# Two layers of attention on 16 images: column sums from chunk probabilities added in place, a step later, and layer 1's weights loaded for each image

## The chip, the cores and the metric

The kernel runs on one core of one Trainium2 chip. The metric is the device time of one execution in microseconds (us), lower is better; the time of a kernel is the median of its runs. A profile is one further execution, taken by the hardware profiler, with its own time.

The engines are named as in the profile: PE (TensorE) with PEld (its weight loads), DVE (VectorE), ACT (ScalarE), POOL (GpSimd) and SP (SyncE, which issues all the large transfers).

## What is computed

The input is 16 images of 64 x 64 pixels and 256 channels, float32. Two residual layers follow each other, each on a group-normalised image:

```python
# layer 0: linear attention over all 4096 pixels, 8 heads of 32
q, k, v = split(gn(x) @ w_qkv)
q = softmax(q, over the head's 32 features) * SCALE
k = softmax(k, over the 4096 pixels)
x = x + (k^T v applied to q) @ w_out
# layer 1: each pixel attends to its 7 x 7 neighbourhood, 8 heads of 32
q, k, v = gn(x) @ Wq + bq, gn(x) @ Wk + bk, gn(x) @ Wv + bv
scores = q . (k of the 49 neighbours + position embedding)
x = x + sum(softmax(scores) * v of the 49 neighbours)
```

The group norm has 32 groups of 8 channels and takes mean and variance over the pixels of an image and the channels of a group. In layer 1 the first four heads have an embedding that depends on one image axis of the neighbour, the other four on the other axis.

## The kernel before, in words

**Stages.** The images are worked on one after the other (the loop at L872). For each image come layer 0 (`layer0`, L500: products with wqkv at L514, the context at L532, output weights, and the residual products at L587), the statistics for layer 1, positional products (L630), `values` (L669, v written to a padded copy in HBM), `keys_queries` for head group 0 (L695), the local attention of head group 0 (L929), `keys_queries` for head group 1 (L930) and the local attention of head group 1 (L953). A head group `hg` is four heads. The instructions of PE, ACT, DVE and SP run in the order in which the program writes them (`manual_schedule`, L860), and POOL's order is left to the scheduler; an engine that waits holds up all that is behind it in its queue.

**Local attention** (`local_attention`, L740). The image is cut into four units of 16 columns (`UNITS`, L41) for each head group, and the 64 rows into nine chunks of 8 key rows (of the padded image). A chunk c of keys meets the query rows `span(c)`, L746: 14 rows for c = 1 to 7, 8 rows for c = 0, 6 rows for c = 8. `scores` (L750) multiplies keys and queries into PSUM (L766) and ACT takes the exponential into a work tile `e` (L774): 128 partitions (8 key rows by 16 key columns, as two halves) by 4 heads x 16 query columns x up to 14 query rows. There is no division by the maximum.

`weighted` (L777) forms, for each half j of the query columns, two sums over the keys (L797): `outs[j]`, the values weighted by e, and `zs[j]`, the plain sums of e, by a product with a block of ones. Each takes four matmuls that lie side by side in four column tiles of PE, one for each head. A query row is met by two chunks, so all these products are added up in PSUM; the four banks are first set to zero by a product with zeros (L784). At the end of a unit `finish` (L805) turns zs (L810), copies outs (ACT, L811), and for each j takes the reciprocal of one column per head (L815, L816), turns it back (L817), multiplies (DVE, L821) and adds the result to the image (POOL, L830). `watch` (L450) adds the sums and reciprocals to running totals on POOL (L451), to find values out of range.

**The order of the steps** is written out by hand in the loop at L832. There are 20 steps, four units i by five groups g of two chunks (the last has one chunk). A step first issues the scores of its own group, then the weighted products of the group before it (`held`), then, if that group ended a unit, the loads of a later unit's values (`load_window`, L728) and `finish`; last `between(i, g)`, which holds the work that belongs to other stages:

- in head group 0 (`between0`, L917): the windows for head group 1, the output stores of a finished unit, the loads of half of the next image, one strip a step (L925), and that half's statistics (`strip_stats`, L473) in units 2 and 3;
- in head group 1 (`between1`, L935): the next image's token tiles, the output stores, the statistics of the other half in unit 1, the group norm's three parts (`group_steps`, L255, with PE products at L266 and L275 and the DVE copies of their results, L268 and L277) in the first three steps of unit 2, and the normalisation of two strips (L283) in unit 3.

The score tiles and the small products of the group norm share two pairs of PSUM banks, taken in turn (`next_bank` gives the next one), so a group-norm product uses a bank that scores need again soon.

**What lies in SBUF.** Wv, Wk, Wq and bv as given stay in SBUF from the start (`wv_sb`, `wk_sb`, `wq_sb`, `bv_sb`). For each image, scaled copies are written to `wv`, `wk` (the tile of `w2`), `wq` and `bv` (`scale`, L601; L892), since the norm's scale is folded into the weights. The work pool has four tiles (L439), which hold e and the intermediate results of other stages. The tail pool has two.

Of the kernel before, what the change touches and what calls it, by code (L numbers as in the profile page):

```python
# [10 lines left out]
F32 = mybir.dt.float32  # L11
# [9 lines left out]
W = 64  # L21
# [67 lines left out]
class Net:  # L89


    def __init__(self, tc, cp, io):
        nc = tc.nc
        self.tc, self.nc, self.cp, self.io = tc, nc, cp, io
        cpk = io["cpk"]

        def tile_of(shape, name):
            return cp.tile(shape, F32, tag=name, name=name)

        self.ident = ident = tile_of([P, P], "ident")  # L100
        make_identity(nc, ident)
        self.grp = tile_of([P, P], "grp")
        nc.sync.dma_start(self.grp, cpk[:, C_GRP : C_GRP + P])
        self.wqkv_sb = tile_of([P, 2, 3 * C], "wqkv")
        self.wout_sb = tile_of([P, 2, C], "wout")
        self.wk_sb = tile_of([P, 2, C], "wk")
        self.wv_sb = tile_of([P, 2, C], "wv")
        for dst, src in ((self.wqkv_sb, "w_qkv"), (self.wout_sb, "w_out"), (self.wk_sb, "wk"), (self.wv_sb, "wv")):
            nc.sync.dma_start(dst, io[src].rearrange("(k p) f -> p k f", p=P))
        self.bk_sb = tile_of([P, 2], "bk")  # L110
        nc.sync.dma_start(self.bk_sb, io["bk"].rearrange("(k p) -> p k", p=P), allow_slow_non_contiguous=True)
        self.bv_sb = tile_of([P, C], "bv")
        nc.sync.dma_start(self.bv_sb, io["bv"].partition_broadcast(P))

        self.ctx_bd = [tile_of([P, P], f"ctxbd{i}") for i in range(2)]
        self.blockdiag = tile_of([P, P], "blockdiag")
        nc.gpsimd.memset(self.blockdiag, 0.0)
        for h in range(4):
            nc.gpsimd.memset(self.blockdiag[HD * h : HD * (h + 1), HD * h : HD * (h + 1)], 1.0)
        self.neghalf = tile_of([P, 1], "neghalf")  # L120
        nc.gpsimd.memset(self.neghalf, -0.5)

    def positions(self, psum):
# [3 lines left out]
        self.wq_sb = cp.tile([P, 2, C], F32, tag="wq", name="wq_sb")  # L127
        nc.sync.dma_start(self.wq_sb, io["wq"].rearrange("(k p) f -> p k f", p=P))
# [5 lines left out]
        with tc.tile_pool(name="setup", bufs=1) as sp:  # L134
            emb_sb = sp.tile([P, 2, KS], F32, tag="emb", name="emb_sb")
            nc.sync.dma_start(emb_sb[:, 0], io["emb0"].rearrange("p a b -> p (a b)"))
            nc.sync.dma_start(emb_sb[:, 1], io["emb1"].rearrange("p a b -> p (a b)"))
            emb_bd = sp.tile([P, 2, 8, 4], F32, tag="embbd", name="emb_bd")
            nc.gpsimd.memset(emb_bd, 0.0)
            wqT = sp.tile([P, 2, C], F32, tag="wqT", name="wqT")  # L140
            for hg in range(2):
                for h in range(4):
                    rows = slice(32 * h, 32 * h + 32)
                    nc.vector.tensor_copy(emb_bd[rows, hg, :KS, h], emb_sb[rows, hg])
                emb = emb_bd[:, hg].rearrange("p a b -> p (a b)")
                pt = psum(f"wqT{hg}")
                for k in range(2):
                    nc.tensor.transpose(pt[:, k * P : (k + 1) * P], self.wq_sb[:, k, hg * P : (hg + 1) * P], self.ident)
                nc.vector.tensor_copy(wqT[:, hg], pt[:, :C])
                for k in range(2):  # L150
                    pe = psum(f"we{hg}{k}")
                    nc.tensor.matmul(pe[:, :32], wqT[:, hg, k * P : (k + 1) * P], emb, start=True, stop=True)
                    nc.vector.tensor_copy(self.wpos[:, k, 32 * hg : 32 * hg + 32], pe[:, :32])
                pb = psum(f"be{hg}")
                nc.tensor.matmul(pb[:32, :1], emb, self.biases[:, 2 + hg : 3 + hg], start=True, stop=True)
                for a in range(2):
                    p0 = 64 * a + 32 * hg
                    nc.vector.tensor_copy(self.biases[p0 : p0 + 32, 4:5], pb[:32, :1])

    def residues(self, psum):  # L160
# [6 lines left out]

        self.stat = tile_of([P, 2, W], "stat")
# [187 lines left out]
def attention_fast(tc, io, ok):  # L356
# [3 lines left out]
    with ExitStack() as ctx:  # L360
# [78 lines left out]
        work = ctx.enter_context(tc.tile_pool(name="work", bufs=4))  # L439
# [35 lines left out]
        def stats_tile(name):  # L475
            return small.tile([P, 2, NS, 6], F32, tag="st", name=name)
# [23 lines left out]
        def layer0(b, x, xn, mean, rstd, xtok, ready):  # L500
# [74 lines left out]
            cT = work_tile(f"cT{b}")[:, :512].rearrange("p (a c) -> p a c", c=P)  # L575
# [23 lines left out]
            return st  # L599

# [139 lines left out]
        def local_attention(b, hg, x, y, vw, after_scores, between):  # L740
# [36 lines left out]
            def weighted(t, c, e, vw):  # L777
                lo, hi = span(c)
                m = 16 * (hi - lo)
                if c == 0:  # L780

                    for i, to in enumerate(single):
                        rows = slice(32 * i, 32 * i + 32)
                        nc.tensor.matmul(to, zb[rows], zb[rows, :1].to_broadcast([32, 512]), start=True, stop=False)  # L784
                for j in range(2):
                    for to in (outs[j], zs[j]):
                        for h in range(4):
                            pl, ab = divmod(h, 2)
                            pr = e[:, ab, pl * m : (pl + 1) * m]
                            dst = to[h * HD : (h + 1) * HD]  # L790
                            if hg == 0:
                                pr = pr.rearrange("p (r w) -> p r w", w=16)[:, :, 8 * j : 8 * j + 8]
                                dst = dst.rearrange("p (r w) -> p r w", w=8)[:, lo:hi]
                            else:
                                pr = pr.rearrange("p (w r) -> p w r", w=16)[:, 8 * j : 8 * j + 8]
                                dst = dst.rearrange("p (w r) -> p w r", w=8)[:, :, lo:hi]
                            nc.tensor.matmul(  # L797
                                dst,
                                ones if to is zs[j] else vw[:, j, c, h * HD : (h + 1) * HD],
                                pr,  # L800
                                start=False,
                                stop=(c == NB - 1),
                            )

            def finish(t):  # L805
                r = [tail.tile([P, 2, 512], F32, tag="tail", name=f"r{b}_{hg}_{t}_{j}") for j in range(2)]
                for j in range(2):


                    nc.vector.transpose(r[j][:, 0], zs[j])  # L810
                    nc.scalar.copy(r[j][:, 1], outs[j])  # L811
                for j in range(2):
# [11 lines left out]
                    for s in (2 * t + j, (2 * t + j + 1) % NS):  # L824
                        for _, p0, m, w, view in pieces(s):

                            a, e = max(w, w0), min(w + m, w0 + 8)
                            if a < e:
                                xv, yv = (view(i[hg][:, strip(s)])[..., a - w : e - w] for i in (x, y))
                                nc.gpsimd.tensor_tensor(yv, xv, by_rows(add[:, :, a - w0 : e - w0], xv), ALU.add)  # L830

            groups = [(i, g) for i in range(4) for g in range(5)]  # L832
            held = None
            for step in range(len(groups) + 1):
# [6 lines left out]
                if held:  # L841
                    i, g, es = held
                    for c, e in es:
                        weighted(UNITS[i], c, e, vw[i])
                    if g == 4:
                        vw.pop(i)
                        if i + 2 < 4:
                            vw[i + 2] = load_window(b, hg, UNITS[i + 2])
                        finish(UNITS[i])
                    between(i, g)  # L850
                held = new


        wm = small.tile([P, 2], F32, tag="wm", name="wm")
        nc.vector.tensor_reduce(wm[:, 0:1], n.wv_sb.rearrange("p a b -> p (a b)"), AX.X, ALU.max, apply_absolute_value=True)
        nc.vector.tensor_reduce(wm[:, 1:2], n.bv_sb, AX.X, ALU.max, apply_absolute_value=True)
# [3 lines left out]
        with tc.manual_schedule(engines=ORDERED):  # L860
# [9 lines left out]
            for s in ORDER[:2]:  # L870
                normalise(xn, x, *gn, s)
            for b in range(B):  # L872
                more = b + 1 < B
                x, xn = halves(b)
                st = layer0(b, x, xn, *gn, xtok, 2)
                mean, rstd = n.group_stats(st, 1e-5, small, bank, f"1_{b}")
# [5 lines left out]
                scale(wv, n.wv_sb, rstd)  # L882
# [9 lines left out]
                nc.vector.tensor_tensor(bv, n.bv_sb, pv[:, :C], ALU.subtract)  # L892
                store_rings()
                for i, s in enumerate(KEYED):
                    values(b, s, x)
                    if i == 1:
                        scale(wk, n.wk_sb, rstd)
                        scale(wq, n.wq_sb, rstd)
# [18 lines left out]
                def between0(i, g):  # L917
                    if g == 4:
                        if i >= 2:
                            vw1[i - 2] = load_window(b, 1, UNITS[i - 2])  # L920
                        store_out(0, i)
# [7 lines left out]
                local_attention(b, 0, x, y, vw, lambda: load_rings(1), between0)  # L929
                keys_queries(b, 1, x)  # L930
                if more:
# [3 lines left out]
                def between1(i, g):  # L935
                    nonlocal steps
                    if g == 4:
                        if more and i >= 2:
                            xtok[i - 2] = load_tokens(b + 1, i - 2)
                        store_out(1, i)  # L940
# [12 lines left out]
                local_attention(b, 1, x, y, vw1, lambda: None, between1)  # L953
# [387 lines left out]
```

## Times and profile before

Of three runs the median is 6052.62 us (6047.84 to 6058.84).

| | |
|---|---|
| profiled execution, its own time | 6068.61 us |
| its span, first to last instruction | 6066.8 us |
| mean granted PE clock | 0.962 of full |
| head group 0's attention, first image | 295.7 to 367.5 us, PE busy 61.69 us |
| keys and queries of head group 1, first image | 367.5 to 395.1 us, PE busy 27.60 us |
| head group 1's attention, first image | 395.1 to 468.2 us, PE busy 63.01 us |
| busy in that stretch: DVE, ACT, POOL | 27.98, 36.49, 15.80 us |
| L797, products with ones, 112 and other columns | 18432 matmuls (records) |
| all transfers | 526.94 MB, 87 GB/s on the average |

How to read it. The page first gives the busy time of each engine as a share of the span, then the queues, and then the chain of work that ended last, followed back from the last instruction to what released it at each step. A group of instructions is shown as line, engine, operation, result <- inputs, partitions x elements and number; behind the first bar its busy time in us and the mean length of one in ns; behind the second the idle time of the engine just before it and what ended most of it. A float32 matmul leaves two records, so the numbers of L766 and L797 are twice those of the program. The waits list what an engine stood still for: the instruction that had to start, the one that released it, the total in us, how often, and the longest. "issue" stands for a wait that ends without any event that the profile has. The granted clock of PE is 1 or 0.5 at any moment; 0.962 is a mean.

### The profile page before, as it was taken

The numbers are of one execution on the slowest core, as the hardware profiler recorded it, in microseconds if no ns is written. First come the engines' busy times: TensorE is split into PE (matmuls) and PEld (weight loads), VectorE is DVE, ScalarE is ACT, GpSimd is POOL, SyncE is SP. The second block draws the span as 40 slices with busy tenths as digits, with TensorE's granted clock in tenths as the row PEclk, the third lists the DMA queues.
The fourth block names the chain that finished last, engine by engine and source line by source line (L and its number), as shares of the span: only waits on it lengthen the run. The fifth ranks groups of instructions, "written<-read, shape, count | busy, mean of one in ns | idle before, by whom it ended". The sixth has DMA issues, their size and how long they took to land.

```text
span 6066.8 us, 171741 instructions
## 1 busy us (share of the span) xinstructions
PE 5506.4 (91%) x76913; PEld 3771.3 (62%) x76913; DVE 2874.6 (47%) x5034; ACT 2254.7 (37%) x3233; POOL 1029.9 (17%) x1945
## 2 busy tenths in 40 slices
PE   3999999898999989999898999999989999898998
PEld 2575665656656566665666657566565665756666
DVE  2544545445354444455444554454544545445354
ACT  0252433515334152342524425143252433415334
POOL 2012120211202113021120201212022120111202
PEclk9999999999999999999999999999999999999999
DMA  4341723516244252443515435163350724417234
GB/s 112 76 104 37 133 80 79 115 45 129 59 96 104 48 121 59 102 104 66 110 44 114 99 74 103 37 129 84 73 112 31 144 66 83 104 39 141 59 76 82
DMA packets 737035, 526.94 MB, mean 87 GB/s; under 512 B 240400, under 2 KB 667664, under 8 KB 733712
## 3 DMA queue, kind: packets, MB, share of 16 engines
q1 hardware_dynamic: 736288, 515.86, 38.9%
q8 instruction: 605, 9.91, 0.7%
q14 instruction: 142, 1.16, 0.1%
HBM read 357.02 MB, written 158.73 MB: 85 GB/s over the span
## 4 chain that ended last, share of the span: by engine, by line
PE 88%; ACT 4%; issue 4%; DVE 2%; SPq 1%; DMA 0%; POOL 0%; ACTq 0%; DVEq 0%; POOLq 0%
PE pd L766 16%; PE ps L797 16%; PE pd L514 15%; PE pd L704 7%; PE ps L532 7%; PE ps L704 5%; ACT qq L619 4%; PE pd L587 4%; PE ps L678 4%; PE pd L678 4%; PE ps L587 4%; PE ps L630 2%; PE ps L546 2%; PE ps L784 1%; SPq L399 1%
## 5 line engine op out<-in xcount | busy, mean ns | idle before, releaser
L774 ACT ACTIVATE e<-pd 128x896 f32<-128x896 f32 (+2 forms) x1152 | 928.5, 839 | 1132.0 <-PE pd L766 1129.4
L766 PE MATMUL pd<-qq,kaug 64*64 64x140 f32 (+5 forms) x27648 | 1052.3, 294 | 218.4 <-ACT e L774 143.5
L766 PEld LDWEIGHTS pd<-qq,kaug 64*64 64x64 f32 x27648 | 923.8, 140 | 354.4 <-issue 163.6
L514 PE MATMUL pd<-wqkv,img 128*128 128x512 f32 x2048 | 923.3, 595 | 1.7 <-DVE img L283 1.6
L797 PE MATMUL ps<-e,vw 128*32 128x112 f32 (+1 forms) x18432 | 853.8, 260 | 63.4 <-issue 63.0
L797 PE MATMUL ps<-e,ones 128*32 128x112 f32 (+1 forms) x18432 | 846.5, 256 | 59.7 <-issue 59.2
L810 DVE STREAM_TRANSPOSE r<-ps 128x512 f32<-128x512 f32 x256 | 168.8, 696 | 1437.6 <-PE ps L797 1437.3
L451 POOL TENSOR_TENSOR others<-others,rc 128x16 f32<-128x16 f32 x256 | 113.1, 442 | 2981.5 <-DVE rc L815 2981.5
L518 ACT ACTIVATE eq<-pd 128x1024 f32<-128x1024 f32 x256 | 261.9, 1023 | 943.3 <-PE pd L514 943.3
L514 PEld LDWEIGHTS pd<-wqkv,img 128*128 128x128 f32 x2048 | 372.6, 191 | 380.6 <-issue 353.3
L797 PEld LDWEIGHTS ps<-e,vw 128*32 128x32 f32 x18432 | 502.9, 113 | 154.9 <-issue 117.7
L797 PEld LDWEIGHTS ps<-e,ones 128*32 128x32 f32 x18432 | 546.5, 114 | 72.4 <-issue 71.8
L619 ACT ACTIVATE qq<-ps,bias 32x512 f32<-32x512 f32 (+2 forms) x544 | 320.2, 622 | 718.1 <-PE ps L630 712.5
L521 DVE TENSOR_REDUCE qz<-eq 128x16 f32<-128x512 f32 x256 | 175.5, 685 | 830.5 <-ACT eq L518 830.5
L532 PE MATMUL ps<-xtok,eq 128*128 128x257 f32 x2048 | 486.1, 380 | 0.0
L532 PEld LDWEIGHTS ps<-xtok,eq 128*128 128x128 f32 x2048 | 386.1, 190 | 149.0 <-issue 107.1
L830 POOL TENSOR_TENSOR img<-img,r 128x320 f32<-128x320 f32 (+1 forms) x512 | 421.5, 844 | 164.8 <-DVE rc L815 163.5
L619 ACT ACTIVATE kaug<-pd,bias 32x512 f32<-32x512 f32 x256 | 173.7, 679 | 633.6 <-PE pd L704 630.7
L473 DVE BATCH_NORM_STATS2 st<-img 128x6 f32<-128x512 f32 x512 | 319.9, 677 | 66.1 <-DMA img<-in_xc 66.1
L621 DVE TENSOR_SCALAR qq<-ps,bias 32x512 f32<-32x512 f32 x384 | 309.3, 806 | 6.8
L524 POOL TENSOR_TENSOR eq<-eq,qr 128x512 f32<-128x512 f32 x256 | 274.7, 1073 | 30.7 <-DVE qr L523 1.2
L821 DVE TENSOR_TENSOR r<-r 128x512 f32<-128x512 f32 x256 | 222.3, 868 | 27.5 <-DVE r L817 0.5
(126 smaller groups left out, 6170.0 us busy)
## 6 DMA issues: line engine op xcount, KB each, us to landing
vw<-vpad SPq DMA_DIRECT2D x512, 288.0 KB
img<-in_xc SPq DMA_DIRECT2D x256, 256.0 KB
xtok<-in_xt SPq DMA_DIRECT2D x64, 1024.0 KB
out<-img SPq DMA_DIRECT2D x256, 256.0 KB
vpad<-v SPq DMA_DIRECT2D x112, 512.0 KB
qq<-pos SPq DMA_DIRECT2D x128, 256.0 KB
qq<-in_ring SPq DMA_DIRECT2D x128, 256.0 KB
pos<-qq SPq DMA_DIRECT2D x128, 112.0 KB
```

What stands on the lines that cost most here:

```text
L473: nc.vector.bn_stats(st[:, k, s], x[k][:, strip(s)])
L514: nc.tensor.matmul(ps[:, t], xn[k][:, n0 : n0 + P], n.wqkv_sb[:, k, : 2 * C], start=(k == 0), stop=(k == 1))
L532: nc.tensor.matmul(pc[hg][:, : C + 1], eq[p][:, t, C + hg * P : C + (hg + 1) * P], xtok[p // 4][:, 2 * (p % 4) + t], start=(p == 0 and t = ...
L587: nc.tensor.matmul(py[co], w2[:, hg, co * P : (co + 1) * P], qq[:, hg, strip(s)], start=(hg == 0), stop=(hg == 1),)
L619: nc.scalar.activation(dst, src, AF.Identity, bias=bias)
L621: nc.vector.tensor_scalar(dst, src, bias, None, ALU.add)
L678: nc.tensor.matmul(pi[:, t], x[k][:, n0 : n0 + P], wv[:, k], start=(k == 0), stop=(k == 1))
L704: nc.tensor.matmul(ps[a], wgt[:, k, hg * P : (hg + 1) * P], x[k][:, strip(pair[a])], start=(k == 0), stop=(k == 1),)
L766: nc.tensor.matmul(to, kaug[pl][rows, u, 8 * c : 8 * c + 8].rearrange("p r w -> p (r w)"), q, start=True, stop=True,)
L774: nc.scalar.activation(e, ps[:, :, : 2 * m], AF.Exp)
L797: nc.tensor.matmul(dst, ones if to is zs[j] else vw[:, j, c, h * HD : (h + 1) * HD], pr, start=False, stop=(c == NB - 1),)
L830: nc.gpsimd.tensor_tensor(yv, xv, by_rows(add[:, :, a - w0 : e - w0], xv), ALU.add)
```

## The change

Four things are changed.

1. **Sums of two chunks.** Two neighbouring chunks c - 1 and c share six query rows. Once both have been read by the weighted products, `both_chunks` adds those six rows of chunk c - 1's e (384 elements for each partition) into chunk c's, in place, on DVE for even c and on POOL for odd c. The product with ones (`summed`) is then made for 8 rows per chunk instead of up to 14 (the six and the two that only chunk c has; 2 rows for c = 0, 6 for c = 8), a step after the weighted products, starts PSUM afresh (so no zeros are needed for zs), and needs each row only once.
2. **The end of a unit.** `finish` is a generator that runs over three steps: the two transposes, then the chain of j = 0, then that of j = 1 with the unit's output stores (`stored`). It starts a step later, and ACT's copies of outs stay where they were. `between` is called a step later. The loop has three more steps at its end.
3. **Weights.** Wv with bv, Wk and Wq are no longer kept in SBUF. They are loaded from HBM for each image (`load_weights`) into the tiles that hold the scaled copies, and scaled in place: Wv and bv during head group 0's attention, Wk after layer 0, Wq after `keys_queries` of head group 1.
4. **Space.** The work pool has six tiles instead of four, the statistics tile one buffer instead of two, and layer 0's `ctx_bd` lies in a work tile.

The core of the diff:

```diff
-        work = ctx.enter_context(tc.tile_pool(name="work", bufs=4))
+        work = ctx.enter_context(tc.tile_pool(name="work", bufs=6))
...
-            return small.tile([P, 2, NS, 6], F32, tag="st", name=name)
+            return small.tile([P, 2, NS, 6], F32, tag="st", bufs=1, name=name)
...
+        def load_weights(to, name):
+            nc.sync.dma_start(to, io[name].rearrange("(k p) f -> p k f", p=P))
+            if name == "wv":
+                nc.sync.dma_start(bv, io["bv"].partition_broadcast(P))
...
+            def both_chunks(c, e, before):
+                r0 = 8 * c - 2 * PAD
+                part = rows_of(c, e, r0, 8 * c)
+                engine = nc.gpsimd if c % 2 else nc.vector
+                engine.tensor_tensor(part, part, rows_of(c - 1, before, r0, 8 * c), ALU.add)
...
-                    for i, to in enumerate(single):
-                        rows = slice(32 * i, 32 * i + 32)
-                        nc.tensor.matmul(to, zb[rows], zb[rows, :1].to_broadcast([32, 512]), start=True, stop=False)
+                    for i, to in enumerate(outs):
+                        rows = slice(64 * i, 64 * i + 64)
+                        nc.tensor.matmul(to, zb[rows], zb[rows, :1].to_broadcast([64, 512]), start=True, stop=False)
                 for j in range(2):
-                    for to in (outs[j], zs[j]):
...
+                    for h in range(4):
+                        v = vw[:, j, c, h * HD : (h + 1) * HD]
+                        products(outs[j], j, h, c, e, *span(c), v, start=False, stop=(c == NB - 1))
+
+            def summed(c, e):
+                r0, r1 = max(8 * c - 2 * PAD, 0), min(8 * c + 8 - 2 * PAD, W)
+                for j in range(2):
+                    for h in range(4):
+                        products(zs[j], j, h, c, e, r0, r1, ones, start=True, stop=True)
...
-            for step in range(len(groups) + 1):
+            held, late, ends, rs, before = None, None, [], {}, None
+            for step in range(len(groups) + 4):
...
                     for c, e in es:
-                        weighted(UNITS[i], c, e, vw[i])
+                        weighted(c, e, vw[i])
                     if g == 4:
+                        rs[i] = [tail.tile([P, 2, 512], F32, tag="tail", name=f"r{b}_{hg}_{i}_{j}") for j in range(2)]
+                        for j in range(2):
+                            nc.scalar.copy(rs[i][j][:, 1], outs[j])
...
-                        finish(UNITS[i])
-                    between(i, g)
-                held = new
+                if late:
+                    i, g, es = late
+                    for c, e in es:
+                        summed(c, e)
+                    if g == 4:
+                        ends.append(finish(i, UNITS[i], rs.pop(i)))
+                if held:
+                    for c, e in held[2]:
+                        if c:
+                            both_chunks(c, e, before)
+                        before = e
+                for end in list(ends):
+                    if next(end, True):
+                        ends.remove(end)
+                if late:
+                    between(*late[:2])
+                held, late = new, held
...
-                scale(wv, n.wv_sb, rstd)
+                scale(wv, wv, rstd)
...
                 def between0(i, g):
+                    if more and i == 0 and g == 0:
+                        load_weights(wv, "wv")
...
-                        store_out(0, i)
...
                 keys_queries(b, 1, x)
+                if more:
+                    load_weights(wq, "wq")
                 if more:
                     load_half(b + 1, 0)
```

`products` is the matmul of L797 for the rows r0 to r1 of a chunk, and `rows_of` the view of those rows in e.

## The prediction, on record before the result

> **What bounds the kernel now.** First the page's busy shares and its chain of work: TensorE (PE) is busy for 91% of the span and carries 88% of the chain, and the two lines of the attention, L766 (scores) and L797 (products with the exponentials), are the two largest entries in it.
>
> ```profile
> PE 5506.4 (91%) x76913; PEld 3771.3 (62%) x76913; DVE 2874.6 (47%) x5034; ACT 2254.7 (37%) x3233; POOL 1029.9 (17%) x1945
> q8 instruction: 605, 9.91, 0.7%
> PE 88%; ACT 4%; issue 4%; DVE 2%; SPq 1%; DMA 0%; POOL 0%; ACTq 0%; DVEq 0%; POOLq 0%
> ```
>
> So a column taken from PE is worth its time, unless PE then waits for something else. How close that is, the waits of PE show (columns: engine and what it did, what ended the wait, us in total, times, longest):
>
> ```profile
> PE pd L766 <- ACT e L774: 143.5, 32, 4.9
> PE ps L797 <- issue: 122.3, 76, 3.4
> PE pd L266 <- DVE gn L263: 120.6, 18, 77.4
> PE pd L766 <- issue: 67.0, 52, 3.3
> PE pd L766 <- DVE gnm L268: 3.8, 15, 0.3
> ```
>
> The first row is the start of each of the 32 attention blocks (one per image and head group), 4.5 us each, behind ACT's evacuations. "issue" is a wait for nothing that the profile names: 189.3 us in 128 waits, four of 1.5 us per block. The group norm for the next image (L268) costs PE 0.3 us a time. Third, the groups of instructions by form, for durations (busy us, mean ns of one):
>
> ```profile
> L797 PE MATMUL ps<-e,vw 128*32 128x112 f32 x14336 | 722.1, 269 | 61.1 <-issue 60.9
> L797 PE MATMUL ps<-e,ones 128*32 128x112 f32 x14336 | 715.0, 266 | 58.4 <-issue 57.9
> L830 POOL TENSOR_TENSOR img<-img,r 128x320 f32<-128x320 f32 x256 | 255.1, 997 | 164.8 <-DVE rc L815 163.5 <-DVE r L821 1.3
> L821 DVE TENSOR_TENSOR r<-r 128x512 f32<-128x512 f32 x256 | 222.3, 868 | 27.5 <-DVE r L817 0.5
> ```
>
> A duration there is a latency, since four heads run in four column tiles at once. The pitch is read from the timeline of one step (start, us, operation): eight records, four heads in two passes, start every 0.192 us at 112 columns, 0.11 at 64 and 0.083 at 48, that is 1.71 ns a column.
>
> ```profile
> 320.99 0.29 PE L797 MATMUL ps<-e,vw 128*32 128x64 f32 x8
> 321.10 0.29 PE L797 MATMUL ps<-e,ones 128*32 128x64 f32 x8
> 321.37 0.69 DVE L821 TENSOR_TENSOR r<-r 128x512 f32<-128x512 f32 x1
> 321.41 0.38 PE L797 MATMUL ps<-e,ones 128*32 128x112 f32 x8
> 321.60 0.38 PE L797 MATMUL ps<-e,vw 128*32 128x112 f32 x8
> 322.14 1.50 POOL L830 TENSOR_TENSOR img<-img,r 128x320 f32<-128x320 f32 x2 [1.32 <-DVE rc L815]
> 323.28 0.90 DVE L821 TENSOR_TENSOR r<-r 128x512 f32<-128x512 f32 x1
> 323.60 0.67 POOL L451 TENSOR_TENSOR others<-others,rc 128x16 f32<-128x16 f32 x1
> ```
>
> Last, the chain of one full step and of one issue wait (start, us, what). A step of two chunks is 1.68 us of scores and 1.67 of products:
>
> ```profile
> 411.74 1.67 PE ps L797 x64
> ...
> 420.93 1.68 PE pd L766 x38
> 422.61 0.70 PE ps L797 x20
> 423.31 2.46 issue
> 425.78 1.54 PE ps L797 x44
> ```
>
> **What the skill says, and whether the trace agrees.** (1) "SBUF — State Buffer", section "Who interferes with whom": a VectorE instruction with two SBUF inputs and a GpSimd instruction that reads SBUF take turns on a shared port, and the later one waits for the whole of the other. The trace agrees: L821 takes 0.69 us alone and 0.90 where it meets L830, and the tiny L451 takes 0.22 us alone (320.38) and 0.67 behind that L821. (2) "Runtime: NRT & Kernel Launch", section "Instruction fetch mechanics": instructions come in blocks of 256, the next while one is executed, the cost "mostly hidden". The block size agrees: q8 moved 605 packets of 16 KB. Hidden it is not: in the trace every issue wait of PE over 0.3 us lies at the same place of a block of 256 PE instructions, 1.3 to 1.8 us after a packet of q8 has ended. (3) "TensorE: Matmul & The Clock Gate", section "What's actually happening": after an idle window of about 3.4 us the clock is halved, and a busy one restores it. The trace shows pieces of 3.4 and 6.8 us at granted clock 0.5, but after shorter gaps: after 2 of 38 gaps of 1.2 to 1.8 us, after 14 of 29 of 1.8 to 2.4, after 23 of 26 of 2.4 to 2.7.
>
> **Part 1, products removed.** A unit has nine chunks, and the ones products now stream, per j, 64 + 7 x 112 + 48 = 896 columns, later 16 + 7 x 64 + 48 = 512. 2 x 384 = 768 columns x 1.71 ns = 1.31 us a unit; 8 units an image, 16 images: 10.5 us an image, 168 us. At a mean granted clock of about 0.94 in the attention (0.95 and 0.93 in two blocks) it is some 10 us more. The matmuls with zeros (L784) go from four of 32 rows to two of 64; both sets run side by side, and I take 0. A step falls from 3.35 to 1.68 + 4 x 0.192 + 4 x 0.11 + 0.13 (turn between kinds) = 3.02 us.
>
> **Part 2, instruction fetch.** The count of PE instructions hardly falls, 224 a full step. So PE uses up 256 in 3.83 us now and in 3.45 afterwards (2.9 at the ends of units). Boundaries that pass just without a wait are 3.4 to 3.5 us apart in the trace, and those where a window or an image strip is loaded about 5.3 (321.79, 327.02, 332.67). At these, four a block, what PE gains is waited for again: 0.4 to 0.6 us each, 1.6 to 2.4; the ordinary boundaries lose their slack and give 0.2 to 0.3 each in the six or so others near a load or a unit's end. I take 3 us a block, 6.1 an image, 98 us. The bounds: 0 if a fetch is faster when asked earlier, 10.5 an image if it is the only limit. The output stores move away from the window loads, which speaks for the lower half.
>
> **Part 3, the adds.** Eight adds of 384 elements a unit, even chunks on DVE, odd on POOL, 512 each in all. No row shows one; it is added work, so no bound lies below nothing. DVE: from 0.292 us at 128 elements (L319) and 0.692 at 512, 0.56 us. POOL: 320 elements take 0.85 to 1.1 and 192 take 0.69, so 0.8 to 1.15. Both engines have room on the average (DVE 28 of 73 us in a block, POOL 16). What counts is their place. The ones products of step n wait for the adds, which can start only when the products of step n - 1 have read the tile, and which stand on DVE behind the transposes and the chain of one j (L815, 0.15; L816, 0.25; L817, 0.71; L821, 0.69 to 1.24: 2 us), on POOL behind two L451 and two L830 (2.2 us). Inside a unit the wait is 1 to 1.5 us on paper, mostly where PE waits for instructions anyway: 0 to 0.5. At the end of a block no scores are left to cover: PE has only c8's products (0.17 us) and c6's and c7's sums (0.44) while DVE does a chain and two adds, 1 to 2.5 us in head group 0, and 2.3 to 3.9 in group 1 where adds read strided rows. In group 1 the group norm adds a wait: L266's PSUM bank comes free by a DVE copy (L268) which now stands behind an add and a chain, 0.56 + 2 us, while the next scores need that bank. PE stalls 1.8 to 2.4 us there instead of 0.3. Less what falls together with instruction waits, I take +0.7 us in group 0 and +3.5 in group 1, 4.2 an image, 67 us; bounds 1.5 and 8 an image.
>
> **Part 4, half clock.** The group-norm stall and the block ends lie at the edge of 1.8 us. Over the 32 blocks a block takes 0.34 us longer for each us at half clock, so a piece of 3.4 or 6.8 us costs 1.2 or 2.3 us. If half of one such stall an image falls over it, 0.5 x 1.7 = 0.8 us an image, 13 us; bounds 0 and 4 an image.
>
> **Part 5, moved steps, at nothing.** Weights: SP issues 384 KB of wv and bv behind the window loads of group 0, needed only after the next image's layer 0; wk after layer 0 (SP waits there for L587), needed about 24 us later; wq after keys and queries of group 1. SP waits for these to end, and the eight strips of the next image's half behind it start 8 us later, in the 4 us in which PE waits for ACT; the statistics want them 20 us later. Uncovered, 640 KB would cost 3 to 4 us an image at the 197 GB/s of the keys and queries. SP's stores of a unit come some 6 us later, after L821 of j = 1, past the window loads and the image strips, which then go one a step; nobody waits for stores but the reuse of y an image later. ACT's copies stay in place. The finish is spread over three steps and starts a step later; its two tail buffers turn over once in 15 us. Six work buffers in place of four: e is held a step longer, and L774 waits for a buffer for 0.9 us in all now, so nothing is gained by them.
>
> **The sum.** -168 - 10 + 98 + 67 + 13 = 0 us against the profiled execution's own 6068.61 (span 6066.8 and 1.8 around it). That execution is 16 us over the median of the three runs, 6052.62; since the sum is a difference I carry it to the median and round for what stayed at nothing: 6055 us. About 0.2%, 12 us, is what measurement of this kernel can tell from no change.
>
> **Rivals.** A, the forecast: the gain goes to instruction waits and to new waits behind the adds; 6015 to 6095, with each cost half way to its bounds. B, faster: the adds hide inside the steps and only fetch takes its share. For it: DVE is at 47% and POOL at 17%, and ACT's order doesn't change. Against it: the port they share. Fetch 4 and waits 3.5 an image: -10.5 - 0.6 + 7.5 = -3.6, x 16 = -58, 5995 us. C, slower: the stalls of group 1 (group norm, end of block) and of group 0's end pass 1.8 us and each brings half clock. Place: the third unit of group 1, where the group norm is, and both block ends. Price: 2.5 stalls x 0.8 x 1.7 = 3.4 us an image in place of 0.8, +42, with 0.5 an image more wait: 6105 us. It decides from the point where DVE's work in front of L268 or of the last add exceeds the cover by 1.8 us. D: the change does not do what it says; the instruction order of the changed kernel has the 64-column products, so I give it nothing.
>
> **How the numbers follow.** A 0.50 (0.15 of it faster by over 0.2%, 0.18 within, 0.17 slower), B 0.28 (all faster), C 0.22 (all slower). Faster 0.43, same 0.18, slower 0.39. Left out are 0.10 of B at the low end and 0.09 of C at the high end: 5985 to 6115. With both signs so near each other, A's own range is 6015 to 6095.
>
> **What would show it.** Part 1: half of the L797 ones records, by another line, at 64 columns and 0.11 us pitch, PE's busy time down by 150 us or more. Part 2: issue waits of L766 and L797 up from 189 to about 290 us. Part 3: a PE wait for the L268 copy of about 2 us 15 times, and waits for the adds at block ends of 1 to 4 us. Part 4: mean granted clock a little under 0.962. Wrong would be: issue waits that do not grow (B), or waits for adds inside the units of over 0.5 us each (then slower than C says).

## The result, and the profile after

The changed kernel takes 6230.27 us (median of 4 runs, 6215.27 to 6245.43) against 6055.73 for the kernel before: a ratio of 1.0291, 95% interval 1.0265 to 1.0317. It is slower by 175 us, where no change was forecast, and outside the range. The profiled execution took 6245.43 us, its span is 6243.6 us, the mean granted clock 0.946.

First the page's busy times and chain of the changed kernel:

```profile
PE 5474.5 (88%) x76657; PEld 3708.4 (59%) x76657; DVE 3325.0 (53%) x5546; ACT 2267.7 (36%) x3233; POOL 1583.3 (25%) x2457
PE 78%; DVE 7%; issue 5%; ACT 4%; POOL 3%; SPq 1%; DMA 0%; DVEq 0%; POOLq 0%; ACTq 0%
```

PE is only 32 us less busy, and its share of the chain falls from 88% to 78%; DVE and POOL, together 2% before, now hold 10%. DVE has 450 us more work, of which the adds are 338. What PE waits for (us in total, times, longest):

```profile
PE ps L814 <- issue: 111.9, 88, 3.8
PE pd L774 <- issue: 83.5, 71, 3.7
PE ps L814 <- DVE e L799: 74.2, 54, 3.6
PE ps L814 <- POOL e L799: 70.2, 74, 2.7
PE pd L774 <- DVE gnm L270: 35.8, 15, 2.6
...
PE ps L814 <- POOL xtok L470: 7.5, 12, 1.1
```

L774 and L814 are the old L766 and L797, L799 is the add, L270 the old L268. The instruction waits are 195.4 us, hardly more than the 189.3 before. New are 144.4 us for the adds and 32 more for the group mean. The last row belongs to the adds too: L470 is a memset of 0.1 us that POOL does directly behind the last add of head group 1, and PE stood waiting for that add before it; with it the waits for adds are 152 us. Now groups of DVE and POOL (busy us, mean ns of one), the last row being that of the kernel before:

```profile
L799 POOL TENSOR_TENSOR e<-e,e 128x384 f32<-128x384 f32 x512 | 539.8, 1054 | 2652.1 <-PE ps L814 2326.6 <-ACT e L782 250.3 <-issue 45.9
L799 DVE TENSOR_TENSOR e<-e,e 128x384 f32<-128x384 f32 x512 | 338.3, 661 | 922.9 <-PE ps L814 582.3 <-ACT e L782 313.3 <-issue 11.5
L844 DVE COPY rc<-r 128x16 f32<-128x16 f32 x256 | 170.7, 667 | 0.0
...
L815 DVE COPY rc<-r 128x16 f32<-128x16 f32 x256 | 40.1, 157 | 1.0
```

The third row is the one to see: the copy of 16 elements at the head of each finish chain (L815 before, 157 ns) now takes 667 ns, though it is the same instruction on operands of the same shape. Sorted by what POOL does as the copy begins, the trace has two kinds: 167 copies begin while a POOL instruction runs and take 940 ns in the mean, the other 89 take 155. In the kernel before not one of the 256 begins while POOL runs. The timeline of a block's end in head group 0 shows why, and how the rest follows (start, us, operation):

```profile
364.34 1.01 POOL L799 TENSOR_TENSOR e<-e,e 128x384 f32<-128x384 f32 x1 [3.41 <-ACT e L782]
364.40 0.98 DVE L844 COPY rc<-r 128x16 f32<-128x16 f32 x1
...
367.22 1.82 POOL L859 TENSOR_TENSOR img<-img,r 128x320 f32<-128x320 f32 x2 [1.25 <-DVE r L850]
367.66 0.86 DVE L799 TENSOR_TENSOR e<-e,e 128x384 f32<-128x384 f32 x1
368.44 0.63 DVE L844 COPY rc<-r 128x16 f32<-128x16 f32 x1
369.00 1.00 POOL L799 TENSOR_TENSOR e<-e,e 128x384 f32<-128x384 f32 x1
...
370.99 1.72 POOL L859 TENSOR_TENSOR img<-img,r 128x320 f32<-128x320 f32 x2 [0.62 <-DVE r L850]
...
372.67 0.99 POOL L799 TENSOR_TENSOR e<-e,e 128x384 f32<-128x384 f32 x1
...
373.71 0.79 PE L814 MATMUL ps<-e,ones 128*32 128x64 f32 x32 [0.95 <-POOL e L799]
```

The copy at 364.40 ends 0.03 us after POOL's add that began before it. The last add on POOL starts as the two image additions (L859) end, and PE's last products start as that add ends. In head group 1 the chain of the changed kernel ends the block behind the normalisation of two strips:

```profile
478.93 1.57 PE ps L814 x80
...
480.72 1.77 DVE img L285 x2
482.49 0.95 DVE e L799
483.44 1.70 DVE img L285 x2
485.15 0.48 DVE e L799
```

**A ledger of PE.** Counted in the traces: the time in which no matmul runs (gaps), half of the time in which one runs at granted clock 0.5 (what half clock costs), and the rest, which is work at full clock. The three add up to the time from PE's first to last matmul. (The first 100 us have no record of the clock; some 10 us of PE's work there count as half clock, in every run.) Before: 543, 196 and 5311 us. After: 752, 285 and 5190. So the 177 us between the two profiled executions are +209 of gaps, +89 of half clock and -121 of work. Each ledger is of one execution, up to 15 us off its kernel's median, so differences of that size between ledgers say nothing.

Per image, the attention of head group 0 goes from 74.5 to 76.7 us and that of head group 1 from 73.5 to 78.9. But the keys and queries after the first go from 27.66 to 28.97 and the rest of the image from 184.6 to 186.5 us with the same gaps: 3.2 us an image, 51 us in all, which is half clock in stages where PE's gaps and its work stay the same.

### The profile page after: what moved, and what is told of

Same layout as the page of the kernel before. It is cut to its first block, busy times and chain, and to the rows that moved or that the text cites. A ratio compares the mean times of both kernels' runs of the same rounds, so it can differ in the third digit from the quotient of the medians.

```text
span 6243.6 us, 172808 instructions
## 1 busy us (share of the span) xinstructions
PE 5474.5 (88%) x76657; PEld 3708.4 (59%) x76657; DVE 3325.0 (53%) x5546; ACT 2267.7 (36%) x3233; POOL 1583.3 (25%) x2457
## 4 chain that ended last, share of the span: by engine, by line
PE 78%; DVE 7%; issue 5%; ACT 4%; POOL 3%; SPq 1%; DMA 0%; DVEq 0%; POOLq 0%; ACTq 0%
PE pd L516 15%; PE pd L774 14%; PE ps L814 9%; PE pd L712 7%; PE ps L534 7%; PE ps L712 5%; ACT qq L627 4%; PE pd L590 4%; PE ps L686 4%; PE pd L686 4%; PE ps L590 4%; PE ps L638 2%; PE ps L548 2%; POOL img L859 2%; DVE e L799 1%
## 5 line engine op out<-in xcount | busy, mean ns | idle before, releaser
L774 PE MATMUL pd<-qq,kaug 64*64 64x224 f32 (+5 forms) x27648 | 1076.3, 297 | 269.7 <-ACT e L782 144.7
L799 POOL TENSOR_TENSOR e<-e,e 128x384 f32<-128x384 f32 x512 | 539.8, 1054 | 2652.1 <-PE ps L814 2326.6
L774 PEld LDWEIGHTS pd<-qq,kaug 64*64 64x64 f32 x27648 | 940.5, 142 | 379.4 <-ACT e L782 152.0
L516 PE MATMUL pd<-wqkv,img 128*128 128x512 f32 x2048 | 950.8, 609 | 1.6 <-DVE img L285 1.6
L799 DVE TENSOR_TENSOR e<-e,e 128x384 f32<-128x384 f32 x512 | 338.3, 661 | 922.9 <-PE ps L814 582.3
L814 PE MATMUL ps<-e,ones 128*32 128x64 f32 (+1 forms) x18432 | 422.5, 223 | 225.4 <-DVE e L799 74.2
L814 PE MATMUL ps<-e,vw 128*32 128x112 f32 (+1 forms) x18432 | 577.8, 263 | 42.9 <-issue 42.1
L859 POOL TENSOR_TENSOR img<-img,r 128x320 f32<-128x320 f32 (+1 forms) x512 | 454.5, 909 | 204.7 <-DVE r L850 145.4
L814 PEld LDWEIGHTS ps<-e,vw 128*32 128x32 f32 x18432 | 420.4, 115 | 135.4 <-issue 96.8
L814 PEld LDWEIGHTS ps<-e,ones 128*32 128x32 f32 x18432 | 342.6, 115 | 263.5 <-DVE e L799 85.2
L453 POOL TENSOR_TENSOR others<-others,qz 128x16 f32<-128x16 f32 x256 | 57.1, 223 | 914.6 <-DVE qz L523 901.7
```

Source lines behind the costliest of these rows:

```text
L516: nc.tensor.matmul(ps[:, t], xn[k][:, n0 : n0 + P], n.wqkv_sb[:, k, : 2 * C], start=(k == 0), stop=(k == 1))
L774: nc.tensor.matmul(to, kaug[pl][rows, u, 8 * c : 8 * c + 8].rearrange("p r w -> p (r w)"), q, start=True, stop=True,)
L799: engine.tensor_tensor(part, part, rows_of(c - 1, before, r0, 8 * c), ALU.add)
L814: nc.tensor.matmul(dst, stationary, pr, **flags)
```

## The experiments

All ratios are to the kernel before, in runs on the same chip. Not all experiments ran on the same chip, so a difference between two of them is taken from their ratios and given in us of the 6055.73. "Port" stands for DVE and POOL shutting each other out, "queue" for waiting behind what stands ahead, "fetch" for my forecast.

**No adds.** In the loop, `if c: both_chunks(c, e, before)` is left out.

> The adds are left out and nothing else: the ones products read the 8 rows of each chunk alone, so every sum lacks the part of the earlier chunk in the six shared rows. Queue theory (PE waits for adds that stand behind the finish chain on DVE and POOL) and port theory (adds and finish steps shut each other out) both say: the 144 us of PE waits for L799 go, the finish's copy of 16 elements falls from 667 ns to about 160, the granted clock returns to 0.96 or more, and the time falls from 6230 to about 5980, under that of before. Fetch theory (my forecast: what the columns gain is waited for again as issue): issue waits rise from 195 to 290 us and the time stays at 6050 to 6100.

Measured: 5996.67 us, ratio 0.9919 (0.9896 to 0.9942). PE's ledger: gaps 615, half clock 175, work 5183. The copy is at 191 ns. So the adds cost 0.0372, 225 us. They cost PE nothing as work (5183 against 5190); all of it is gaps and half clock. Both the port and the queue theory stand. Fetch has its part, for issue waits are now 248 us, 59 more than before, but not the 290 of the forecast:

```profile
PE ps L814 <- issue: 153.9, 127, 4.1
PE pd L774 <- issue: 94.2, 84, 3.6
```

**Group norm first.** In unit 2 of head group 1 `between` is called ahead of the adds and of `finish`:

```diff
+                norm = late and late[0] == 2 and late[1] < 3 and hg == 1
+                if norm:
+                    between(*late[:2])
...
-                if late:
+                if late and not norm:
```

> The group norm's three parts are issued ahead of the adds and the finish chain of their step. Queue theory: PE's wait for the copy of the group mean falls from 35.8 us to about 5, with less half clock after it: about 6185. If what is late next is the add behind it, PE waits there for the same time: 6215 to 6235.

Measured: 6192.62 us, ratio 1.0244 (1.0218 to 1.0270). The wait for the mean falls from 35.8 to 3.8 us, the one for the variance rises from 4.9 to 18.4, half clock falls by 43 us (in the ledger, 285 to 242, of a profiled execution that lies 15 us under the median). By the ratios the edit is worth 0.0047, 28 us. The queue did this.

**All adds on DVE.** `engine = nc.vector`.

> All adds on DVE, none on POOL. Port theory: the copy of 16 elements (667 ns) and the adds (661 ns) fall towards 200 and 560 ns, PE no longer waits for POOL (70 us), DVE waits grow by less than that: about 6180. Queue theory: DVE has 512 adds more, 290 us, ahead of and behind the finish chain, PE's waits for DVE grow from 74 by more than 70 us: 6240 to 6300.

Measured: 6227.09 us, ratio 1.0293 (1.0267 to 1.0319), no change. The copy falls to 176 ns and no wait for POOL is left, but the waits for adds on DVE rise from 74.2 to 116.4 and the issue waits from 195.4 to 217.6 us (a group of instructions, then a wait):

```profile
L844 DVE COPY rc<-r 128x16 f32<-128x16 f32 x256 | 45.0, 176 | 0.0
...
PE ps L814 <- DVE e L799: 116.4, 109, 4.2
```

What the port gives, the fuller queue of DVE and the instruction waits take: neither expectation holds alone.

**The copy as a reduction.**

```diff
-                    nc.vector.tensor_copy(rc[:, 0], turned[:, :, 0])
+                    nc.vector.tensor_reduce(rc[:, 0], turned[:, :, 0:1], AX.X, ALU.max)
```

> The finish's copy of 16 elements is made by a reduction over one element, which should not meet POOL on the port; nothing else moves. Port theory: the row falls from 667 to about 200 ns, the DVE chain is 0.45 us shorter twice a unit, of which PE sees a half to all at the ends of units: 6110 to 6180. Queue theory: the place in the queue decides and not the 0.45 us: 6210 to 6235. If the reduction is shut out too, the row stays over 500 ns and the time at 6230.

Measured: 6152.87 us, ratio 1.0173 (1.0148 to 1.0199): 0.0118 or 71 us from one instruction of 16 elements. Its row in this run, with the adds still on both engines:

```profile
L844 DVE TENSOR_REDUCE rc<-r 128x16 f32<-128x16 f32 x256 | 42.7, 167 | 0.0
```

667 to 167 ns, 128 us of DVE; PE's waits for adds fall from 152 to 98 us (the 14.4 at L470 counted in). In the ledger gaps fall by 41 and half clock by 68: the larger part of the gain is half clock. In this run 171 of the 256 reductions begin while a POOL instruction runs, and these take 171 ns in the mean. This is the port. The Trainium skill states it ("SBUF — State Buffer", section "Who interferes with whom"): a copy can enter a mode with both ports and then contends with GpSimd, a reduction on this chip never does. The copies and the reductions that began beside a running POOL instruction, 940 and 171 ns, agree with both halves of that.

**Short adds.** One of the six shared rows is added, `rows_of(c, e, r0, r0 + 1)`.

> Each add takes one of the six shared rows instead of six (64 elements for 384), so the sums lack five rows of the earlier chunk; every add, wait and place in a queue stays. If length and port time decide: the waits for L799 fall by two thirds or more and the time comes to 6010 to 6070, near that without adds (5997). If the place in the queue decides (a wait for the chain in front, however short the add): 6120 to 6200.

Measured: 6093.99 us, ratio 1.0051 (1.0032 to 1.0071), between the two expectations. The waits for adds fall to 33 us. Of the 3.7% between no adds (0.9919) and the changed kernel (1.0291), 2.4% is the length of five rows in six, and 1.3% is what remains: the sixth row, the place in the queue and the waits that come with it, which this run does not separate. Half clock is still 225 in the ledger against 175 without adds.

**The weights only.** The kernel before with everything of the change but the attention loop.

> The kernel before with the weights loaded for each image, six work tiles and one statistics tile, and nothing else. My part 5 put that at nothing: within 12 us of the kernel before. Rival: the reload holds up SP and the transfers, 3 to 4 us an image: 50 to 65 us slower, which would be a third of the 175.

Measured: 6059.98 us, ratio 1.0009 (0.9996 to 1.0022). The reload, with the six work tiles, costs nothing that can be told: the interval ends at 0.2%, 13 us.

**Three undoings together**, the adds on both engines and then on DVE: the reduction, the group norm first, and

```diff
-                    if i == 3 and g in (1, 2):
-                        normalise(xn_next, x_next, *gn, ORDER[g - 1])
+                    if i == 2 and g >= 3:
+                        normalise(xn_next, x_next, *gn, ORDER[g - 3])
```

> Three undoings together, adds still on both engines: the copy of 16 elements as a reduction (-77 alone), the group norm ahead of the adds (-38 alone), and the normalisation of two strips moved from the last unit of head group 1 to the end of the one before it. If they are independent: 6230 - 77 - 38 = 6115, less up to 4 us an image at the block's end, 6050 to 6115. If each only uncovers the next wait: 6120 to 6150.

> The same three with all adds on DVE, so that no add stands behind the image additions of POOL. In the chain of the run with the reduction, units end with an add on POOL behind two such additions, 2.7 us. If that is what is left: 20 to 50 us below the split version, 6020 to 6080. If DVE is too full with 512 adds more: 10 to 60 above it.

Measured: 6136.81 us, ratio 1.0129 (1.0109 to 1.0148), and 6126.52 us, 1.0105 (1.0086 to 1.0124). The first is what the two known edits give together (1.0291 - 0.0118 - 0.0047 = 1.0126); if these two add up, the normalisation moved brings nothing that can be told. Its place at the block's end is taken: in head group 1 PE now waits there for POOL's two image additions and the last add behind them, 1.2 to 2.7 us in each of 15 images. The trace puts this down to the memset behind that add:

```profile
PE ps L814 <- POOL xtok L470: 31.6, 15, 2.7
```

With all adds on DVE PE still waits 77 us for them, and the time is only 10 us lower, less than the 20 to 50 expected. There the chain at the ends of head group 0's blocks holds the next image's statistics and the adds.

**No adds at the block's end.** In the last of four units the chunks 6 to 8 are not added; the ones products run over all their rows, into zs set to zero. Once on top of the last version, once as the only edit of the changed kernel.

```diff
+            def added(i, c):
+                return 0 < c < NB and (i < 3 or c < 6)
...
+                r1 = min(8 * c + 8 - 2 * PAD, W) if added(i, c + 1) else span(c)[1]
...
-                        if c:
+                        if added(held[0], c):
```

> The version with all adds on DVE and the three undoings, and in each block's last unit the chunks 6, 7 and 8 are not added: their ones products run over all their rows, into zs set to zero. That costs PE 3 x 0.16 = 0.5 us a block. Block-end theory: the 3 to 4 us at each block's end (adds behind statistics and behind each other) go, with the half clock after them: -2.5 us a block, 80 us, to 6040 to 6060, near the kernel before, perhaps under it. If PE then waits for the statistics or for instructions instead: 6090 to 6120.

> The changed kernel with this edit alone. Block-end theory: PE waits for L799 fall by 1 to 3 us in each of 32 blocks, 6130 to 6180. If most of the waits lie inside the units: 6200 to 6230.

Measured: alone 6089.03 us, ratio 1.0083 (1.0054 to 1.0112), which is 0.0208, 126 us or 3.9 us a block, more than expected. Ledger: gaps 647 (-106), half clock 203 (-82), work 5211 (+21). The keys and queries are back at 27.66 us, the rest of the image at 184.4. PE's waits for adds in this run:

```profile
PE ps L814 <- POOL e L799: 42.3, 54, 2.1
...
PE ps L814 <- DVE e L799: 2.9, 10, 0.5
```

On top of the other edits: 6018.98 us, ratio 0.9962 (0.9951 to 0.9972), below the 6040 to 6060 expected. This version beats both kernels, by 0.4% and, by the two ratios, about 3%. In it the adds are nearly covered (14.7 us of waits), and instruction waits are up by 28 us on before:

```profile
PE ps L814 <- issue: 132.5, 120, 3.6
...
PE pd L774 <- issue: 84.6, 77, 4.0
...
PE ps L814 <- DVE e L799: 14.7, 26, 1.3
```

**No window loads.** The version without adds, with `vw[i + 2] = vw.pop(i)` in place of `load_window`.

> The version without adds, and in the attention the third and fourth unit use the windows of the first two, so that these 256 transfers of 288 KB are not made (values and sums are then not those of the reference). If the issue waits are instruction fetches slowed by window loads: of 248 us some 60 to 100 go, and the time falls from 5997 to about 5910 to 5940. If they come at every 256 instructions whatever else is moved: within 15 us of 5997.

Measured: 5816.05 us, ratio 0.9622 (0.9594 to 0.9650), 0.0297 or 180 us below the version without adds, more than twice the expected. No window was waited for there, and yet PE's issue waits fall from 248 to 116 us:

```profile
PE ps L814 <- issue: 74.7, 94, 3.2
PE pd L774 <- issue: 41.0, 55, 2.1
```

The gaps fall by 135 in the ledger, half clock by 28. The instruction waits of over 0.3 us that are left lie within eight of whole multiples of 256 PE instructions apart, weight loads counted, and all but at most one in a trace end 1.0 to 1.8 us after a packet of the instruction queue q8; so do those of the kernel before, of the changed kernel and of the version without adds. So it is the window loads that lengthen the waits at the boundaries of 256 instructions, as the forecast had read from their spacing. They are not the only cause: 116 us stay without window loads.

## Why the prediction was wrong, point by point

**The columns (part 1, -168 and -10): size.** The work of PE at full clock fell by 121 us, and by 128 without adds, so the adds aren't the reason. PE's busy time, forecast to fall by 150 or more, fell by 32, for half clock counts in it (-121 + 89). A full step went from 1.67 to 1.35 us, 0.32 against 0.33 in the sum; the loss is in the others. Eight records at 16 columns take 0.061 us in the trace where 1.71 ns a column gives 0.027, and c8's sums, now in a step with the next unit's first products, add a turn between kinds. I have not split the 47 us further.

**Instruction fetch (part 2, +98): right mechanism, too large, and not added to the other waits.** It measured +6 in the changed kernel and +59 where the adds are gone, so part of the 98 was never there. Without window loads the growth is gone too (116 us against 189 before). That it is +6 beside the adds is read so: PE, held up by adds, no longer comes early to the boundaries. The runs fit this, for the issue waits are 195 us with the adds, 219 with the reduction, 257 with short adds and 248 without any. I added fetch and engine waits, having taken off only what I thought fell together; in the changed kernel nearly all of fetch falls together. Issue waits that do not grow were the forecast's sign of B, the faster rival; they came with a slower kernel.

**The adds (part 3, +67): the step that failed.** PE's waits grew by 184 us, 11.5 an image where the forecast had 4.2: 152 for adds and 32 for the mean, and half clock came on top. The lengths were right: in the trace the median add takes 0.56 us on DVE and 1.02 on POOL, forecast 0.56 and 0.8 to 1.15, and the wait for the mean is 2.4 us, the upper end of 1.8 to 2.4. Three terms were not.

First, the deduction for what falls together with instruction waits. In the trace 106 us of the waits for adds lie in the last 7 us of the blocks, 2.4 us a block in head group 0 and 4.2 in head group 1. The prices of the block ends before the deduction, 1 to 2.5 and 2.3 to 3.9, were about right. But in the kernel before, the instruction waits in the last 7 us of the blocks are 17 us in all, 1 us an image, so there was little to fall together with. The chain there also has links that I listed but priced one at a time: an add on POOL behind two L859, which wait for a chain, which waits for a copy, which waits for an add. Without the adds at the block ends the kernel gains 7.8 us an image (126 / 16), half clock included.

Second, the waits inside the blocks, put at nothing in the sum. They are 46 us in 57 waits, 0.8 us each, and this was the sign that the forecast had named for "slower than C says".

Third, the copy. The prediction knew the port and priced it on L821 and L451, but took the 16-element copy from its row (L815, 0.15 us) as if it could not be shut out, because before it never met POOL. With POOL busy as it began it took 0.94 us, at the head of each chain that the adds stand behind: 0.0118 or 71 us, waits and half clock together.

**Half clock (part 4, +13): size.** It is +89 by the ledger, 51 of it in stages behind the blocks, which I had not counted at all. The price was low too: over the same 32 blocks of the kernel before, a line fitted to each block's time against its time at half clock rises by 0.54 us for each us, where the prediction says 0.34. In six of the versions half clock goes roughly with the gaps: 752, 724, 711, 669, 647, 615 us of gaps stand beside 285, 242, 217, 225, 203, 175. Their sum alone doesn't settle it, for the kernel before has fewer gaps, 543 us, and 196 of half clock. In the changed kernel all 126 stretches of half clock begin within 3.5 us after the end of a gap of over 0.9 us. That a gap near a block's end causes the half clock of the next stage is inferred from this and from the run without adds at the block's end, in which the keys and queries are back at 27.66 us; no run made a gap by itself.

**The moved steps (part 5, 0): right** for the weights and the space, at 1.0009. The moved finish and stores were tried only together with the sums.

**The rival C** had the sign and the places, block ends and group norm, but priced them at +50.

## What to carry to other kernels

Work taken from the busiest engine is paid back wherever the replacement stands in an ordered queue behind something long and in front of nothing that covers it: leave the replacement out at the ends of a stage, where the cover ends, even if it is sound in the middle (here leaving out the 3 last of 32 adds a block gave back 126 of the 225 us that all adds cost). Before putting work on GpSimd, look for every VectorE copy or two-input instruction that will now meet it, the tiny ones at the head of a chain first; their present duration says nothing of that. Before taking off a wait because another falls together with it, look in the trace whether the other stands in that place: here it mostly didn't at the block ends. And removing one wait can show the next, as the instruction waits did here when the adds were gone.

## What the runs showed of the hardware

A copy of 16 elements on DVE took 155 ns in the mean where no POOL instruction ran as it began, 940 where one did, and as a reduction 171 beside a running POOL instruction. "Mostly hidden" ("Runtime: NRT & Kernel Launch", section "Instruction fetch mechanics") does not hold where a full step of 224 small PE instructions takes 3.03 us (1.68 of scores and 1.35 of products) while windows are loaded: 132 us of waits went with 256 transfers. Half clock was paid after gaps much shorter than 3.4 us, in the changed kernel after 18 of 33 gaps of 1.8 to 2.4 us, and often in the next stage: 3.2 us an image in stages whose own gaps had not changed.
